# A fused scan-and-attention kernel: normalising the first chunk's second half sooner, and starting the projections ahead 22 slots later

## The chip, the cores and the metric

The kernel runs on one core of a Trainium2 chip. A core has a matmul engine (TensorE, PE in the views; its weight loads are PEld), a vector engine (VectorE, DVE), an activation engine (ScalarE, ACT), a general engine (GpSimd, POOL), and a queue engine (SyncE, SP) that mainly issues transfers. ACT issues transfers too. Each engine runs its own instructions in order and waits on semaphores for the others. The metric is the device time of the whole launch in microseconds (us).

## The reference

Input x has 32 sequences of 256 tokens with 256 features; a condition vector has 512 features for each sequence. First a selective scan is computed, then two layers of local attention and a gated feed-forward, and x is added at the end.

```python
xr, gate = split(x @ W_in.T)            # 512 + 512 channels
xc = silu(causal_conv4(xr + cond))      # per channel, along tokens
xn = layernorm(xc)                      # over the 512 channels
Bm, Cm, dt = split(xn @ W_xproj.T, 3)   # 16 states each
Ad = 1 - tanh(A_log) * 0.01 * tanh(dt @ W_dt.T + b_dt)
Bd = Bm * minimum(norm(xn), 1)
h  = clip(h * Ad + Bd * xn, -10, 10)    # one step for each token
y  = Cm . h + D * xn
x1 = (y * silu(gate)) @ W_out.T
x2 = two layers of attention and feed-forward on x1
out = x + x2
```

## The kernel before, in words

The 32 sequences are taken as NG = 4 groups of GB = 8. The scan of a group goes through NCH = 8 chunks of CH = 32 tokens. In a step of the scan (`step`, L722) DVE updates a 128 x 512 state h (16 states x 8 sequences on the partitions, 512 channels along a row) for one token of eight sequences. There are 256 steps for a group.

A chunk needs much before its first step. `project` (L401) multiplies x with the input weights, `conv_in` and `conv_taps` (POOL L480, DVE L474 and L491) do the convolution and `conv_th` (L501) the silu. `raw_sums` (L520) forms the raw B, C and dt sums. Then each chunk is normalised in NJ = 2 halves of 128 rows:

- `norm_turn` (PE L550) transposes a half into `tp_x`;
- `norm_stats` (DVE L560 to L569, POOL L567) takes mean and variance and raises the variance to the power -0.5;
- `norm_shift` and `norm_apply` (ACT L574, L581) write the normalised rows `xn`;
- `norm_affine` (POOL L588, L589) multiplies and adds the learnt scale and shift;
- `norm_put` (SP L599) writes the half to `xnd` in device memory; `norm_out` (ACT L594) sums the squares.

`length` (DVE L605, POOL L606) takes the norm of both halves, `figures` and `figures_out` (DVE L615, PE L624) spread the statistics, `figures_in` and `decays` turn them into the factors `beta`, the limits of the clip and so on. In the first group, rows for the steps come in two ways: `load_skip` (SP L751) loads `xq` from `xnd`, and `spread_rows` (PE L699) copies two of every eight tokens from it to all partitions as `bx`; the others are loaded by `load_rows` (SP L691), 256 KB each, as `xrep`. `scale_row` (ACT L712) multiplies by beta. `read_out` (PE L734) sums h with C for four tokens into `y`.

The scan of the first group runs nearly alone, before any attention. Beside it the kernel projects x for the later groups ("ahead"): 48 units u, each with `ahead_load` (SP L417, two transfers of 128 KB into `xa` for every second unit), `ahead_project` (PE L428, four matmuls into `ps_a`, eight rows of the profile), `ahead_copy` (ACT L439) and `ahead_put` (SP L444, 256 KB to `ahead`). From slot 220 or so they are all done, and later groups only load them (`xp`).

Order: each piece of work is put into a slot with `at(slot, what, ...)`. Slot 0 is the first step, and a step takes one slot. `scan_slots` runs the slots in order; within a slot one list comes before the other. The program is then built by a scheduling layer that may shift instructions of one engine past each other, so that a change of slots also moves other work, such as the weight loads (L985), which have no inputs to wait for. Once built, the order on each engine is fixed. A transfer uses one of eight semaphores in turn, so its issue can also wait for the transfer eight before it.

In the startup, small constants are folded too: `widen_w` (POOL L292) writes `wide`, `sum_w` (PE L303) sums it into `tw`, `sums_w` (DVE L312 to L314) copies `wsum` and `wbias`.

After slot 274 the first group is done, and attention and feed-forward of a group run beside the scan of the next group.

Of the kernel before, what the change touches and what calls it, by code (L numbers as in the profile page):

```python
# [27 lines left out]
CH = 32  # L28
NCH = S // CH
# [44 lines left out]
def kernel(  # L74
# [149 lines left out]
    def program(ctx, exact):  # L224
# [154 lines left out]
        def group_scan(g):  # L379
# [8 lines left out]
            alone = g == 0  # L388
# [5 lines left out]
            def at(s, what, *args):  # L394
                agendas[-1].setdefault(s, []).append(partial(what, *args))
# [289 lines left out]
            def by_tensor(t):  # L685
                return alone and t % (2 * NQ) < XR
# [175 lines left out]
            for c in range(NCH):  # L862
                s0 = c * CH
                for hb in range(CH // TB):
                    s = s0 + hb * TB
                    for i in range(NI):
                        at(s + 4 * i + 5, read_out, c, hb, i)
                    at(s + 21, gated, c, hb)
                    at(s + 25, out_gate, c, hb)
                    at(s + 11, skip, c, hb)  # L870
                for ch in range(NC_):
                    at(s0 - 38 + 2 * ch, conv_in, c, ch)
                    at(s0 - 37 + 2 * ch, conv_taps, c, ch)
                    at(s0 - 36 + 2 * ch, conv_th, c, ch)
                    if not alone:
                        at(s0 - 35 + 2 * ch, conv_out, c, ch)
                for ch, s in enumerate((13, 16, 17, 18)):
                    at(s0 + s + 2, gate_th, c, ch)
                    if not alone:
                        at(s0 + s + 4, gate_out, c, ch)  # L880
                at(s0 - 25, raw_copy, c)
                at(s0 - 24, raw_turn, c)
                for j in range(NJ):
                    s = s0 - 26 + 4 * j
                    at(s + 2, norm_stats, c, j)
                    at(s + 5, norm_shift, c, j)
                    at(s + 5, norm_apply, c, j)
                    at(s + 6, norm_affine, c, j)
                    at(s + 9, norm_out, c, j)
                    at(s + (9 if alone else 10), norm_put, c, j)  # L890
                at(s0 - 11, length, c)
                at(s0 - 9, figures, c)
                at(s0 - 7, figures_in, c)
                at(s0 - 6, decay_th, c)
                at(s0 - 5, decays, c)
                at(s0 - 4, put_c, c, 0)
                at(s0 + 4, put_c, c, 1)
                for d in range(KM):
                    at(s0 + 45 + 2 * d, copy_y, c, d)
                    at(s0 + 46 + 2 * d, put_y, c, d)  # L900
            agendas.append({})
            for c in range(NCH):
                s0 = c * CH
                at(s0 - 43 if alone else s0 + 6, load_x, c)
                if alone:
                    for ch in range(NC_):
                        at(s0 - 40 + 2 * ch, project, c, ch)
                else:
                    for i in range(2):
                        at(s0 - 44 + 2 * i, load_projected, c, i)  # L910
                for ch, s in enumerate((13, 16, 17, 18)):
                    at(s0 + s, project, c, NC_ + ch)
                at(s0 - 27, raw_sums, c)
                for j in range(NJ):
                    at(s0 - 26 + 4 * j, norm_turn, c, j)
                at(s0 - 8, figures_out, c)
                for t in range(CH):
                    if not by_tensor(t):
                        at(s0 + t - 6, load_rows, c, t)
                    if by_tensor(t) and t % XR == 0:  # L920
                        at(s0 + t - 4, spread_rows, c, t)
                    at(s0 + t - 2, scale_row, c, t)
                for hb in range(CH // TB):
                    s = s0 + hb * TB
                    at(s - 9 if alone else s + 7, load_skip, c, hb)
                    at(s + 23, out_turn, c)
                for d in range(KM):
                    at(s0 + 43 + 2 * d, project_y, c, d)

            if alone:  # L930
                n = (NG - 1) * NCH * 2
                for u in range(n):
                    s = -30 + u * (NCH * CH) // n
                    at(s - 5, ahead_load, u)
                    at(s, ahead_project, u)
                    at(s + 2, ahead_copy, u)
                    at(s + 4, ahead_put, u)
            return agendas

        def scan_slots(groups):  # L940


            slots, scans = {}, [group_scan(g) for g in groups]
            for part in range(2):
                for i, agendas in enumerate(scans):
                    for s, what in agendas[part].items():
                        slots.setdefault(i * S + s, []).extend(what)
            for s in range(min(slots), max(slots) + 1):
                for what in slots.get(s, ()):
                    what()  # L950
                yield s
# [613 lines left out]
        s0 = done[0]  # L1565
# [130 lines left out]
```

## Time and profile before

| | us |
|---|---|
| median of 3 runs | 3534.11 |
| lowest, highest | 3530.09, 3535.70 |
| the profiled execution | 3535.63 |
| its span, first to last instruction | 3533.5 |
| PE busy in the span | 3418.2 (97%) |
| DVE busy | 2683.2 (76%) |
| ACT busy | 2035.4 (58%) |
| POOL busy | 1625.6 (46%) |

The profile's page gives for each engine the time in which it was busy, the same in 40 slices, the DMA queues, the chain of waits followed back from the last instruction, and the costliest groups of instructions. A row such as `L722 DVE CUSTOM_DVE_ANT_0 h<-h,xrep,lim` names the line of the kernel, the engine, the operation, and output and inputs by their names in the program. In rows in order of time the first number is the start and the second the duration, both in us; `x4` counts instructions, and the bracket tells how long the engine was idle before and what ended that. `SPq` and `ACTq` are issues of transfers. Busy PE time is modelled in part, and a PE that waits between the parts of a matmul can count as busy.

### The profile page before, as it was taken

The numbers are of one execution on the slowest core, as the hardware profiler recorded it, in microseconds if no ns is written. First come the engines' busy times: TensorE is split into PE (matmuls) and PEld (weight loads), VectorE is DVE, ScalarE is ACT, GpSimd is POOL, SyncE is SP. The second block draws the span as 40 slices with busy tenths as digits, with TensorE's granted clock in tenths as the row PEclk, the third lists the DMA queues.
The fourth block names the chain that finished last, engine by engine and source line by source line (L and its number), as shares of the span: only waits on it lengthen the run. The fifth ranks groups of instructions, "written<-read, shape, count | busy, mean of one in ns | idle before, by whom it ended". The sixth has DMA issues, their size and how long they took to land.

```text
span 3533.5 us, 56484 instructions
## 1 busy us (share of the span) xinstructions
PE 3418.2 (97%) x19580; PEld 2257.4 (64%) x19580; DVE 2683.2 (76%) x5177; ACT 2035.4 (58%) x3663; POOL 1625.6 (46%) x1587
## 2 busy tenths in 40 slices
PE   7999989999999999999999999999999999999999
PEld 4545335666666666666666666666666777777777
DVE  5888898878788788888888888888787655555563
ACT  4666656656666665666666656666566444444442
POOL 4433456544455555544455555544444434333441
PEclk9999999999999999999999999999999999999999
DMA  7787655545454555444454555544444212011111
GB/s 208 215 217 218 198 169 153 136 113 142 129 143 130 150 147 151 136 114 134 117 142 128 148 148 147 137 120 130 118 142 118 61 37 62 13 31 36 37 28 38
DMA packets 487195, 436.65 MB, mean 124 GB/s; under 512 B 247155, under 2 KB 326516, under 8 KB 486772
## 3 DMA queue, kind: packets, MB, share of 16 engines
q1 hardware_dynamic: 401426, 420.41, 42.2%
q10 hardware_dynamic: 85474, 12.53, 2.1%
q8 instruction: 157, 2.57, 0.3%
q14 instruction: 138, 1.13, 0.1%
HBM read 384.06 MB, written 47.19 MB: 122 GB/s over the span
## 4 chain that ended last, share of the span: by engine, by line
PE 63%; DVE 17%; DMA 7%; POOL 5%; ACT 4%; issue 3%; SPq 1%; ACTq 0%; DVEq 0%; POOLq 0%
PE ps_qkv L996 13%; PE pa L1405 13%; DVE h L722 7%; PE po_f L1432 6%; PE y L734 5%; PE ps_wo L1052 4%; PE ov L1289 3%; DMA xrep<-xnd 3%; PE ps_out L814 3%; PE ps_in L401 3%; PE sc L1232 3%; PE tr_qk L1041 2%; PE rs L1269 2%; PE ps_raw L520 2%; DVE acc L491 1%
## 5 line engine op out<-in xcount | busy, mean ns | idle before, releaser
L722 DVE CUSTOM_DVE_ANT_0 h<-h,xrep,lim 128x512 f32<-128x512 f32 x1024 | 917.2, 896 | 137.3 <-ACT xrep L712 93.4
L712 ACT ACTIVATE xrep<-xrep,beta 128x512 f32<-128x512 f32 x960 | 671.6, 719 | 265.5 <-DMA xrep<-xnd 178.2
L996 PE MATMUL ps_qkv<-qkv,res 128*128 128x512 f32 x1536 | 716.0, 601 | 26.6 <-DVE ag L1423 12.5
L1405 PE MATMUL pa<-hT,w 128*128 128x256 f32 (+1 forms) x2816 | 674.7, 382 | 5.1 <-DVE zT L805 5.1
L1405 PEld LDWEIGHTS pa<-hT,w 128*128 128x128 f32 (+1 forms) x2816 | 517.4, 188 | 145.4 <-issue 41.8
L1020 POOL TENSOR_TENSOR rot<-rot,swp 128x512 f32<-128x512 f32 x256 | 345.1, 1348 | 496.7 <-DVE swp L1017 465.9
L996 PEld LDWEIGHTS ps_qkv<-qkv,res 128*128 128x128 f32 x1536 | 282.0, 191 | 311.5 <-issue 247.0
L1026 POOL TENSOR_TENSOR rn<-ss,neg_half 128x8 f32<-128x8 f32 x256 | 457.6, 1788 | 0.0
L734 PE MATMUL y<-h,ly 128*32 128x512 f32 x2048 | 341.1, 606 | 15.7 <-DVE h L722 13.6
L1432 PE MATMUL po_f<-ag,w 128*128 128x256 f32 x1280 | 306.7, 387 | 3.8 <-DVE fo L1443 3.1
L1423 DVE SCALAR_TENSOR_TENSOR ag<-pa,b_sb,ag 128x256 f32<-128x256 f32 x320 | 151.5, 474 | 208.7 <-ACT ag L1416 208.7
L1009 ACT ACTIVATE sq<-ps_qkv,tiny 128x512 f32<-128x512 f32 x256 | 173.3, 685 | 186.3 <-PE ps_qkv L996 129.3
L1432 PEld LDWEIGHTS po_f<-ag,w 128*128 128x128 f32 x1280 | 235.3, 190 | 68.3 <-DVE pT L1260 12.9
L1416 ACT ACTIVATE ag<-pa,b_sb 128x256 f32<-128x256 f32 x320 | 150.0, 469 | 209.7 <-PE pa L1405 206.8
L1357 POOL TENSOR_TENSOR rstd<-ve,neg_half 128x2 f32<-128x2 f32 x64 | 46.5, 726 | 484.9 <-DVE ve L1355 484.8
L1052 PE MATMUL ps_wo<-oT,wo 128*128 128x256 f32 x1024 | 231.6, 379 | 0.0
L1012 DVE TENSOR_TENSOR rot<-ps_qkv,rc_sb 128x512 f32<-128x512 f32 x256 | 175.1, 684 | 71.8 <-ACT sq L1009 70.1
L491 DVE SCALAR_TENSOR_TENSOR acc<-xr,wc_sb,acc 128x256 f32<-128x256 f32 x384 | 183.1, 499 | 50.8 <-POOL acc L480 50.0
L1017 DVE TENSOR_TENSOR swp<-ps_qkv,rs_sb 128x256 f32<-128x256 f32 x512 | 191.8, 416 | 27.6 <-POOL rot L1020 27.5
L1052 PEld LDWEIGHTS ps_wo<-oT,wo 128*128 128x128 f32 x1024 | 194.5, 190 | 27.2 <-ACT th_g L774 0.8
L1032 DVE SCALAR_TENSOR_TENSOR rot<-rn,rot 128x512 f32<-128x512 f32 x256 | 205.7, 841 | 7.5 <-POOL rn L1026 7.5
L1244 ACT ACTIVATE pT<-sc 128x512 f32<-128x512 f32 x384 | 201.6, 601 | 8.2 <-PE sc L1232 6.1
(161 smaller groups left out, 5375.6 us busy)
## 6 DMA issues: line engine op xcount, KB each, us to landing
xrep<-xnd SPq DMA_DIRECT2D x960, 256.0 KB
rb<-inv SPq DMA_DIRECT2D x128, 256.0 KB
xnd<-xn SPq DMA_DIRECT2D x64, 256.0 KB
qkv<-in_wqkv_dram SPq DMA_DIRECT2D x24, 512.0 KB
ahead<-xs_a SPq DMA_DIRECT2D x48, 256.0 KB
xp<-ahead SPq DMA_DIRECT2D x48, 256.0 KB
xd<-xnd SPq DMA_DIRECT2D x192, 64.0 KB
w<-in_w_dram SPq DMA_DIRECT2D x80, 128.0 KB
```

The costliest lines, as they stand in the source:

```text
L491: nc.vector.scalar_tensor_tensor(acc, xr[:, :, k : k + CH], wc_sb[:, ch, k : k + 1], acc, ALU.mult, ALU.add,)
L712: scaled = nc.scalar.activation(bx, ck[c].pop(("bx", t), bx), AF.Copy, scale=ck[c]["beta"][:, t : t + 1])
L722: nc.vector._custom_dve(TENSOR_ADD_SAT, out=h_new, in0=state["h"], in1=bx, s0=ck[c]["lim"][:, 0, t : t + 1], s1=ck[c]["lim"][:, 1, t : t + 1],
L734: nc.tensor.matmul(ck[c]["y", hb][32 * q : 32 * q + 32, :], ly[hb % 2][:, 32 * t : 32 * t + 32], ck[c].pop(("h", hb * TB + t)), start=(i = ...
L996: nc.tensor.matmul(ps, res[b][:, k, t0 : t0 + W], wt["qkv", a][:, k], start=(k == 0), stop=(k == KM - 1),)
L1020: nc.gpsimd.tensor_add(rot, rot, swp)
L1026: nc.gpsimd.tensor_tensor(rn, ss, neg_half, ALU.pow)
L1032: nc.vector.scalar_tensor_tensor(rot, bc(rn, 2, DH), 1e12, rot, ALU.min, ALU.mult)
L1052: nc.tensor.matmul(po[:, d], wt["wo", 0][:, c, d * P : (d + 1) * P], oT[:, c, :], start=(c == 0), stop=(c == NC_ - 1),)
L1244: nc.scalar.activation(p, banks[r], AF.Exp)
L1405: nc.tensor.matmul(dst[x], wt["w1", m][:, k, x], self.h[:, k], start=(k == 0), stop=(k == KM - 1),)
L1432: nc.tensor.matmul(self.po[:, d], wt["w2", 0][:, m, d * P : (d + 1) * P], self.ag[m], start=(m == 0), stop=(m == len(MCH) - 1),)
```

## The change

Two edits, both for the first group alone (`alone`):

1. In the first chunk (c = 0) the second half's normalisation is placed 1 slot behind the first half's, not 4. This moves `norm_turn`, `norm_stats`, `norm_shift`, `norm_apply`, `norm_affine`, `norm_out` and `norm_put` of j = 1 by 3 slots to the front.
2. The 48 units of projections ahead begin at slot -8, not -30, and are spread over 234 slots, not 256. Load, copy and put move with each unit.

```diff
                 for j in range(NJ):
-                    s = s0 - 26 + 4 * j
+                    s = s0 - 26 + (1 if alone and c == 0 else 4) * j
                     at(s + 2, norm_stats, c, j)
...
                 for j in range(NJ):
-                    at(s0 - 26 + 4 * j, norm_turn, c, j)
+                    at(s0 - 26 + (1 if alone and c == 0 else 4) * j, norm_turn, c, j)
...
                 n = (NG - 1) * NCH * 2
                 for u in range(n):
-                    s = -30 + u * (NCH * CH) // n
+                    s = -8 + u * (NCH * CH - 22) // n
                     at(s - 5, ahead_load, u)
                     at(s, ahead_project, u)
                     at(s + 2, ahead_copy, u)
                     at(s + 4, ahead_put, u)
```

In the built programs the order of instructions differs on every engine up to the end of the first group's scan and is the same after it.

## The prediction

> **What bounds the kernel now.** All times are from one profiled execution: 3535.63 us, of which the span from first to last instruction is 3533.5 us. The median of the three runs shown is 3534.11 us, so I work out a difference and add it to either; my forecast is given against the median.
>
> I read the page's slices first: TensorE is busy nine tenths everywhere but in the first 40 us and in the slice around 470 us. So the first scan (group 0, before attention starts near 490 us) has a start-up with idle engines and then a stretch in which TensorE is nearly full. The busy time by stretch shows both; the columns are from:to, length, then busy us and instructions of PE, PEld, DVE, ACT, POOL, then clock, DMA share and GB/s.
>
> ```profile
> 18.00:42.00 24.00, 19.73 (x111) 15.65 (x110) 7.53 (x23) 8.64 (x19) 12.48 (x20) 0.93 0.78 225
> 100.00:381.00 281.00, 266.82 (x1201) 145.98 (x1200) 243.81 (x417) 184.96 (x341) 109.12 (x144) 0.95 0.80 218
> ```
>
> The reader is to see 266.82 of 281 us of PE in the second row (95%), DVE at 87%, DMA at 80%. Who bounds it is told by the chain of waits of that window alone:
>
> ```profile
> by line: PE ps_a L428 15.1%; PE y L734 14.8%; DMA xrep<-xnd 10.6%; DVE h L722 9.5%; PE ps_in L401 9.1%; PE bx L699 7.8%; PE ps_out L814 6.8%; PE ps_raw L520 4.3%; issue 4.1%; ACT xrep L712 3.5%; DMA xq<-xnd 3.2%; PE tp_x L550 2.3%; DMA xp<-
> ```
>
> The seven PE terms sum to 60%; ps_a, the projection that the change moves, is the largest of all. Its rows before the first step (40) and in the full stretch (285):
>
> ```profile
> L428 PE MATMUL ps_a<-xa,w_in_sb x40: 379/379/483, 18.6 to 40.0; 128*128 128x256 f32 x40
> L428 PE MATMUL ps_a<-xa,w_in_sb x285: 379/379/634, 99.7 to 380.9; 128*128 128x256 f32 x143
> ```
>
> Eight rows are one unit u, so 5 units run before the first step and 36 in the stretch. The start-up, in order of time:
>
> ```profile
> 28.65 0.70 DVE L560 BATCH_NORM_STATS2 st<-tp_x 128x6 f32<-128x512 f32 x1 [3.72 <-PE tp_x L550]
> 31.89 0.63 PE L550 MATMUL tp_x<-ident,xc 128*128 128x128 f32 x4
> 33.17 1.97 PE L428 MATMUL ps_a<-xa,w_in_sb 128*128 128x256 f32 x8
> 34.88 0.61 POOL L292 COPY wide<-wx 128x512 f32<-128x512 f32 x1
> 37.20 1.26 POOL L588 TENSOR_TENSOR xn<-xn,lng_sb 128x512 f32<-128x512 f32 x1 [1.71 <-ACT xn L581]
> 38.55 1.26 POOL L589 TENSOR_TENSOR xn<-xn,lnb_sb 128x512 f32<-128x512 f32 x1
> 39.84 0.34 SPq L599 DMA_DIRECT2D xnd<-xn  x1
> 40.59 0.17 DVE L605 TENSOR_SCALAR ss<-ss 128x2 f32<-128x2 f32 x1 [3.31 <-ACT sq_x L594]
> 41.99 0.66 PE L624 MATMUL ps_st<-rhs,sel 128*128 128x96 f32 x4 [1.61 <-DVE rhs L615]
> 43.76 2.83 SPq L751 DMA_DIRECT2D xq<-xnd  x4
> 48.71 0.81 DVE L722 CUSTOM_DVE_ANT_0 h<-h,xrep,lim 128x512 f32<-128x512 f32 x1 [0.45 <-POOL xr L473]
> 48.75 2.08 PE L401 MATMUL ps_in<-xg,w_in_sb 128*128 128x256 f32 x4
> 52.95 1.03 PE L401 MATMUL ps_in<-xg,w_in_sb 128*128 128x256 f32 x4
> 53.00 0.80 DVE L722 CUSTOM_DVE_ANT_0 h<-h,xrep,lim 128x512 f32<-128x512 f32 x1
> ```
>
> It shows the first half's statistics at 28.65, the second half's transposes 3.2 us later at 31.89, the second half's row write at 39.84, its length at 40.59, the first step at 48.71 and the second at 53.00. The whole stretch counts: after the first scan the order of every engine is the same in both built programs, and PE is busy 2654 of 2700 us from 600 to 3300. What the first scan gains or loses moves the end by as much.
>
> **The change, part by part.**
>
> *Second half earlier.* In the built order the second transposes follow the first after one tw group (0.95 us), so they end at about 28.62 + 0.95 + 0.63 = 30.2 instead of 32.5. But the later engines serialise. DVE now does both bn_stats and both aggregates before either half's variance leaves: 30.2 + 0.70 + 2 x 0.18 + 0.15 + 0.14 + 0.15 = 31.7. POOL then does two powers (0.58 each), two wide copies (0.61 each) and four passes of 1.26 with gaps of 0.08: the passes start at about 33.9 and end at 39.2. So the first half's write slips from 34.43 to about 36.5, and the second's comes at 39.2 instead of 39.84: 0.6 us gained. The third wide copy, at 34.88 before, now stands behind the passes: 39.2 + 0.61, then its tw matmuls (0.95), then the three wsum copies (0.4), which stand ahead of the length on DVE. The length starts at about 41.3 instead of 40.59: 0.7 us **lost**. So what needs the figures (ps_st, beta) is 0.7 us late and the row write 0.6 us early.
>
> *Row loads.* The SP queue of before has 3.92 us between the second write (39.84) and xq (43.76); in the built order of before xq also waits for a matmul that reads an xa buffer, and in the new one it does not. I cost the gain from 0 (xq was not last) to 2.0 us. Then comes the first step: in the new DVE order it stands behind two taps of the next chunk's third channel, where the second step stood (53.00). So the first step gets later, about 52, and the next ones find their work done; by the fifth step (57.24) I count both orders as equal. Queued on SP ahead of the first write now are all weight loads, the 768 KB one included. Its price is 0 if it has landed by 36; six loads took 7.80 us at 23.40, so eight more issues at 1.3 us from 31 end at 41.4, 2.2 us after the write is due. Four small-run xa transfers and five 256 KB puts leave the same stretch, so I take 0. Start-up sum: from -4.0 (write 0.6, xq 2.0, and 1.4 from a lighter queue, that being xa's own issue of 8.99 us for six) to +2.9 (0.7 + 2.2); I take 0.
>
> *Projections later.* 48 units now lie 4.875 slots apart instead of 5.33, from slot -8. Five leave the idle start-up; in PE's order one of them stands between ps_st and the first bx, the rest among the steps. In 100 to 381 that is 36 x (5.333/4.875 - 1) = 3.4 units more, and 1.6 more between 42 and 100. Price of one: at most its whole 1.97 us, if PE never waits: 5 x 1.97 = 9.9 us. At least what a unit now adds to the chain: 15.1% of 281 us by 36 units is 1.18 us, and from 53 to 100 ps_a is 6.5% of the chain for 7 units, 0.44 us: 3.4 x 1.18 + 1.6 x 0.44 = 4.7 us. PE's 95% speaks for the upper end, its 60% of the chain for the lower; y and bx also count waits for h and xq as busy. I take the mean, **+7.3 us**. Each unit's ACT copy (0.57 us) and SP put move with it; I cost them at nothing here, since ACT is busy 185 of 281 us; if ACT were full they would add 5 x 0.57 = 2.9.
>
> *DMA.* Five puts (256 KB) and four xa loads (128 KB) enter the step time; the 768 KB and 42 KB weights leave it. That is 1.0 MB at 218 GB/s, 4.6 us of transfers; xrep and xq hold 13.8% of the chain: **+0.6 us**. Whole cost 4.6, if rows always ended last; 0 if never.
>
> Sum: 0 + 7.3 + 0.6 = **+7.9 us**, about 3543.5 for the profiled execution and 3542 for the median.
>
> [...]
>
> **Rivals.**
>
> *The start-up wins, not slower (-6 to +3.5).* Place: PE between bx and the ninth step. If write, xq and the clock all gain (-4.0 and up to 2.0 for bx and ps_in run warm) and extra units fall in PE's waits at 0.44 us each (2.2), the sum is -3.8: 3530. For it: PE idles 14 of 281 us, and y rows stretch while waiting for h. Against: ps_a heads the chain. It decides if the ninth step starts 3 us or more before its present 61 us.
>
> *Rows and order win, clearly faster.* xrep waits hold 10.6% of 281 us, 30 us. If the new order of puts and loads takes a third of them off, -10, with the rest at +3: 3527. For it: single waits of 5 us; against: more transfers in the stretch.
>
> *Everything is paid in full.* 9.9 for PE, 4.6 for DMA, 2.9 for the start: +17.4, 3551. For it: PE 95%, DMA 80%. Against: some of these overlap.
>
> *It does not do what it says:* the second half's figures come no earlier, since POOL and DVE serialise. That is in my forecast.
>
> **How the numbers follow.** Forecast +3.5 to +13: 0.52. Start-up wins: 0.27. Rows win: 0.13. Paid in full: 0.08. A difference of 0.2% (7.1 us, about what a measurement of this kernel can tell from no change) splits the forecast: 0.36 of it above. Faster by over 0.2%: 0.13 + 0.03 of the start-up case = 0.16. Slower: 0.36 + 0.08 = 0.44. Same: 0.40. The range leaves out about one in ten on each side: 3530 to 3549; the forecast's own is 3537 to 3547.
>
> **What would show it.** Right: no ps_a before about 43 us; second write near 39, length near 41; fifth step within 1 us of 57.2; then each 50 us holds about half a step less, PE busy over 96% from 100 to 381, the last ps_a near 389. Wrong: the ninth step well before 58, or the step rate unchanged at 1.52 us with more units in it (then units are free), or the end moving by other than the first scan's shift.

## The result and the profile after

The changed kernel takes 3547.23 us (median of 6 runs, 3543.48 to 3549.49), the kernel before 3531.64 us beside it (6 runs, 3530.09 to 3535.70): a ratio of 1.0036, with a 95% interval of 1.0024 to 1.0048, or 12.7 us more. The two medians alone lie 15.6 us apart, a quotient of 1.0044, which is inside that interval; the text goes by the ratio as recorded. The profiled execution took 3549.49 us, of which the span is 3547.2 us: 13.7 us more than the span of before.

The busy time by stretch, in the same columns as before:

```profile
18.00:42.00 24.00, 13.61 (x64) 11.17 (x64) 6.71 (x21) 5.40 (x13) 12.08 (x20) 0.63 0.69 200
100.00:381.00 281.00, 264.16 (x1197) 143.60 (x1196) 238.55 (x412) 181.84 (x335) 112.24 (x145) 0.98 0.82 216
```

In the start-up PE does 64 matmuls where it did 111, and the granted clock is 0.63 where it was 0.93. In the full stretch PE is busy 264.16 of 281 us; it was 266.82. The units are denser there, and yet PE is idle longer; but a second profile of the kernel before (before_again, below) has 262.77, so that difference is no more than lies between two executions of one kernel. The chain of waits of that stretch:

```profile
by line: PE ps_a L428 13.9%; PE y L734 13.4%; DMA xrep<-xnd 12.7%; DVE h L722 10.4%; PE ps_in L401 8.7%; PE ps_out L814 4.6%; issue 4.4%; PE bx L699 4.3%; ACT xrep L712 3.9%; PE ps_raw L520 3.8%; POOL acc L480 2.6%; PE tp_x L550 2.3%; DVE a
```

ps_a has less of the chain than before (13.9% after 15.1%), the row loads (xrep) and the steps (h) have more. This too is no effect of the change: in before_again, the same order as before, the same stretch has

```profile
by line: DMA xrep<-xnd 18.8%; DVE h L722 12.8%; PE ps_a L428 11.5%; PE y L734 10.7%; PE ps_in L401 6.6%; issue 4.7%; PE bx L699 4.5%; PE ps_out L814 4.1%; ACT xrep L712 4.0%; PE ps_raw L520 3.5%; DMA ys<-yo 3.3%; POOL acc L480 3.0%; DMA xq<
```

so even the line that heads the chain changes from one execution to the next. The units' rows, from 40 to 410 us, with the first and last start:

```profile
L428 PE MATMUL ps_a<-xa,w_in_sb x384: 379/379/634, 45.5 to 401.8; 128*128 128x256 f32 x192
```

No unit runs before 45.5, and the last ends near 402, 20 us later than before. The start-up in order of time (start, duration, and in brackets the idle time before and what ended it):

```profile
36.00 2.89 SPq L599 DMA_DIRECT2D xnd<-xn  x2
39.15 1.87 PE L303 MATMUL tw<-wx,wide 128*128 128x2 f32 x8 [2.67 <-POOL wide L292]
41.05 0.16 DVE L312 COPY wsum<-tw 128x3 f32<-128x3 f32 x1 [9.77 <-PE tw L303]
41.39 0.16 DVE L605 TENSOR_SCALAR ss<-ss 128x2 f32<-128x2 f32 x1
42.78 1.14 PE L624 MATMUL ps_st<-rhs,sel 128*128 128x96 f32 x4 [1.77 <-DVE rhs L615]
43.71 1.97 PE L401 MATMUL ps_in<-xg,w_in_sb 128*128 128x256 f32 x4
55.20 0.81 DVE L722 CUSTOM_DVE_ANT_0 h<-h,xrep,lim 128x512 f32<-128x512 f32 x1
```

The two row writes are issued as one group from 36.00; the last tw group takes 1.87 us instead of 0.95, and behind it stand wsum and the length, at 41.39; ps_st takes 1.14 us instead of 0.66, the first four rows of ps_in 1.97 instead of some 1.0; the first step is at 55.20.

Where the time went is read best from the starts of the steps (the rows of L722). Against the first profile of before the changed kernel is 3.5 us late at the ninth step, 6.6 at the 17th, 8.7 at step 184, 7.8 at step 204, 15.5 at step 224, and 14.4 at step 256. So the loss does not grow evenly with the steps; it comes at the start, between steps 12 and 16, and between steps 204 and 224. The end of the first scan carries it on: the first matmul of attention starts 15.4 us later, the span ends 13.7 us later.

### The profile page after: what moved, and what is told of

Read it like the earlier page. It is cut to its first block, busy times and chain, and to the rows that moved or that the text cites. A ratio compares the mean times of both kernels' runs of the same rounds, so it can differ in the third digit from the quotient of the medians.

```text
span 3547.2 us, 56509 instructions
## 1 busy us (share of the span) xinstructions
PE 3424.2 (97%) x19580; PEld 2257.8 (64%) x19580; DVE 2684.6 (76%) x5177; ACT 2037.2 (57%) x3663; POOL 1629.2 (46%) x1587
## 3 DMA queue, kind: packets, MB, share of 16 engines
q14 instruction: 138, 1.13, 0.1%
## 4 chain that ended last, share of the span: by engine, by line
PE 63%; DVE 17%; DMA 7%; POOL 5%; ACT 4%; issue 3%; SPq 0%; ACTq 0%; DVEq 0%; POOLq 0%
PE ps_qkv L996 14%; PE pa L1405 13%; DVE h L722 7%; PE po_f L1432 6%; PE y L734 5%; PE ps_wo L1052 4%; PE ov L1289 3%; DMA xrep<-xnd 3%; PE sc L1232 3%; PE ps_in L401 3%; PE ps_out L814 3%; PE tr_qk L1041 2%; PE rs L1269 2%; DVE acc L491 2%; PE ps_raw L520 2%
## 5 line engine op out<-in xcount | busy, mean ns | idle before, releaser
L722 DVE CUSTOM_DVE_ANT_0 h<-h,xrep,lim 128x512 f32<-128x512 f32 x1024 | 914.5, 893 | 142.8 <-ACT xrep L712 100.6
L734 PE MATMUL y<-h,ly 128*32 128x512 f32 x2048 | 356.3, 609 | 18.3 <-DVE h L722 17.6
```

The lines of the kernel that those rows point to most:

```text
L722: nc.vector._custom_dve(TENSOR_ADD_SAT, out=h_new, in0=state["h"], in1=bx, s0=ck[c]["lim"][:, 0, t : t + 1], s1=ck[c]["lim"][:, 1, t : t + 1],
L734: nc.tensor.matmul(ck[c]["y", hb][32 * q : 32 * q + 32, :], ly[hb % 2][:, 32 * t : 32 * t + 32], ck[c].pop(("h", hb * TB + t)), start=(i = ...
```

## The experiments

The names of the theories in the expectations: **A**, the cold TensorE clock of the start-up; **B**, my prediction's, that a unit among the steps is paid as PE time; **C**, that the loss is a matter of the order on the queues at a few places; **D**, that edit 1 loses the start. All runs are compared by ratio with the kernel before on the same chip, since its median there lay between 3531.64 and 3540.24 us. In one list, with the ratio turned into us by 3535:

| kernel | units: first slot, spread | ratio [95%] | us |
|---|---|---|---|
| after | -8, 234 | 1.0036 [1.0024, 1.0048] | +12.7 |
| after_again | -8, 234 | 1.0031 [1.0019, 1.0042] | +11.0 |
| warm | -8, 234 | 1.0035 [1.0023, 1.0047] | +12.4 |
| late_only | -8, 234 | 1.0023 [1.0012, 1.0033] | +8.1 |
| spread_238 | -8, 238 | 1.0025 [1.0014, 1.0036] | +8.8 |
| spread_252 | -8, 252 | 1.0027 [1.0017, 1.0036] | +9.5 |
| late_wide | -8, 256 | 1.0001 [0.9990, 1.0012] | +0.4 |
| dense_early | -30, 234 | 1.0022 [1.0013, 1.0031] | +7.8 |
| half_only | -30, 256 | 1.0000 [0.9991, 1.0009] | 0.0 |
| sparse_drift | -30, 278 | 1.0010 [0.9997, 1.0023] | +3.5 |
| before_again | -30, 256 | 1.0001 [0.9989, 1.0012] | +0.4 |
| put_act | -8, 234 | 1.0007 [0.9997, 1.0016] | +2.5 |
| before_put_act | -30, 256 | 0.9985 [0.9971, 1.0000] | -5.3 |

late_only, before_again and before_put_act have the second half of before (four slots), the others that of the change (one slot).

**Each edit alone.** half_only keeps edit 1 and takes edit 2 back:

```diff
-                    s = -8 + u * (NCH * CH - 22) // n
+                    s = -30 + u * (NCH * CH) // n
```

> Edit 1 alone: second half one slot behind the first, the 48 units as before (from slot -30, over 256 slots). Theory A (cold TensorE: without the five units between the start-up chains the clock falls, and each short chain is paid double): the units are back, so the start keeps its clock; ps_st near 0.7 us, the fifth step near 57.2 us, total within 2 us of the kernel before. Theory B (my prediction: five units that cost nothing in the start-up are paid among the steps): also within 2 us. Theory C (the late units meet the next group's loads near slots 184 to 220): also within 2 us. Rival D (the second half's passes push the last wide copy, wsum and with it the length back by 0.8 us, and that is the start's loss): fifth step 3 us late, total +3 or more.

Measured 1.0000: edit 1 alone costs nothing, and D falls. late_only has edit 2 without edit 1 (`s = s0 - 26 + 4 * j` in both places):

> Edit 2 alone: the second half stays four slots behind the first, the 48 units begin at slot -8 and are spread over 234 slots. Theories A, B and C: the whole loss is here, +10 to +15 us against the kernel before. Theory A adds: first ps_st over 1 us and granted clock under 0.7 from 18 to 42 us, fifth step 2 us late or more. Rival D (edit 1 is what loses the start): at most +9, and a fifth step near 57.2.

Measured +8.1 us, under the 10 to 15 that A, B and C had: some two thirds of the loss belong to edit 2 by this number, and the interval (4 to 12 us) reaches nearly all of it. It holds D's bound of 9 too, but half_only has settled D.

**The clock.** warm adds to the kernel after five units of matmuls whose result nobody reads:

```diff
+                for s in (-30, -25, -20, -15, -10):
+                    at(s, warm)
```

> The kernel after with five dummy units on TensorE alone at the slots that lost a unit (-30, -25, -20, -15, -10): eight rows each of the input weights by themselves into a bank that nobody reads; no transfer, no copy, and the outputs are not changed. Theory A: the clock from 18 to 42 us is back near 0.93, ps_st near 0.7, first ps_in near 1.0, fifth step near 57.2, and the total 3.5 to 6 us below the kernel after (3541 to 3544). Theories B and C: the start is not the cause, total as after (3546 to 3549). If the start's 3.3 us come from elsewhere (wsum behind the passes), step times up to the fifth are as in the kernel after.

The start came out as A has it, the total did not. The same stretches in warm:

```profile
18.00:42.00 24.00, 19.39 (x103) 15.15 (x103) 6.71 (x21) 6.14 (x14) 11.69 (x19) 0.86 0.65 192
42.00:53.00 11.00, 11.00 (x52) 8.88 (x51) 7.09 (x22) 3.18 (x7) 6.17 (x14) 1.00 0.62 160
```

The clock is back at 0.86 and 1.00, and the ninth step starts at 63.1 us. In the five profiles with edit 1, units from slot -8 and the puts on SP, but no filler, it starts at 64.2 to 66.5 (mean 65.6). But the whole kernel is at 1.0035, as the kernel after. So the cold clock costs some 2.5 us at the start, by one profile, and is not what costs 12.

**Density.** dense_early has the spacing of the change from the old first slot:

```diff
-                    s = -8 + u * (NCH * CH - 22) // n
+                    s = -30 + u * (NCH * CH - 22) // n
```

> Edit 1, and the units as dense as in the kernel after (one in 4.875 slots) but from slot -30, so that the last stands near slot 199. Five units stand in the start-up again. Theory B (PE is full, a unit among the steps is paid wherever it stands): about as before, -2 to +2. Theory C (late units collide with the next group's loads from slot 212): also no late loss, and rather faster than before, -2 to -6, since before has its last units at slot 220. If density itself were the loss (too many transfers and matmuls a step), steps 16 to 190 would each be slower, by up to 7 us in all, and given back after slot 199.

Measured +7.8 us. B and C both had it at before or better; only the case named last in the expectation, that density itself is the loss, had a loss of that size and place. Its profile loses 1.6 us at steps 12 to 16 and 8.0 from 16 to 184, nothing at 204 to 224, and gives 2.6 back from step 184 to 256, where that case had all of it given back. The next runs were chosen to part the number of units from the order. late_wide begins late but has the old spacing:

```diff
-                    s = -8 + u * (NCH * CH - 22) // n
+                    s = -8 + u * (NCH * CH) // n
```

> Edit 1, and the units from slot -8 but as far apart as in the kernel before (256 slots), so that they end at slot 242: five units stand in steps that had none, and no step has more than before. Theory B: the five are paid as in the kernel after, +7 to +12. Theory C: in the built order xp stands ahead of the xq loads, as in the kernel before, so the loss at steps 212 to 216 is gone; start +3, five units in steps that are not full of PE work about +2 (by 46.9 us for 32 steps without units against 48.4 with six, 0.25 each, to 0.44), total +4 to +6.

Measured 1.0001, or +0.4 us with an interval from -4 to +4: under C's 4 to 6, whose lower end it just reaches. Five units moved out of the start-up, to the steps behind slot 220, cost nothing that can be told. That is against B's +7 to +12 for five displaced units; it does not test the denser spacing, which late_wide does not have. spread_252 then changes one number of late_wide, 256 to 252, and with it the order on SP:

```diff
-                    s = -8 + u * (NCH * CH) // n
+                    s = -8 + u * 252 // n
```

> The kernel of run late_wide with 252 in place of 256: the units begin at slot -8 and lie 5.25 slots apart instead of 5.33, so the number of units in any stretch is the same to one, and the last stands at slot 238. In the built SP order, though, 50 xq loads stand ahead of the last chunk's x (xg) and 58 ahead of the next group's first xp, as in the kernel after (51 and 58); in late_wide and in the kernel before it is 48 and 56. Theory C (order on SP: x and xp come 3 steps late and PE and DVE, whose orders hold their readers, stand): the losses at steps 184 to 188 (+3) and 212 to 216 (+4 to +5) are there, total 6 to 9 us above late_wide, 1.0017 to 1.0026 of before. Theory B (so many units among the steps, each paid as PE time): as late_wide, 1.000 with 0.001 either way.

Measured 1.0027 against 1.0001, with intervals that do not touch: 9 us between two kernels whose unit counts are the same to one in any stretch. So 9 us can be lost without denser units. In the profiles 5.9 us of the difference come from step 204 to 224 (7.1 against 1.2), as C had it; the other loss that C forecast, at steps 184 to 188, is not there (0.2).

**Where the order costs: steps 212 to 216.** spread_238 changes 234 to 238 in the kernel after:

> The kernel after with one number changed: the 48 units from slot -8 are spread over 238 slots, not 234 (the last at slot 225, not 221). Up to slot 35 every unit stands where it stands in the kernel after; in the built order the next group's first load (xp) then stands on SP ahead of the xq loads of the last chunk but one, as it does in the kernel before, and not behind two of them. Theory C (the late loss is SP's order: xp is issued 3 steps later, and DVE, whose order holds the add of xp at step 216, waits 3.4 to 5.0 us for it where it waited 1.0): steps 212 to 216 take 6.6 us again, not 12, and the total falls by about 4, to 3542 to 3544. Theory B (each unit is paid as PE time wherever it stands among the steps): as the kernel after. The start should repeat that of the kernel after: +3 us at the fifth step, and the further 3.5 us at steps 12 to 16 if that is no accident of one execution.

The issues of SP around step 213, in the kernel before:

```profile
372.82 0.54 SPq L449 DMA_DIRECT2D xp<-ahead  x1
374.09 1.38 SPq L751 DMA_DIRECT2D xq<-xnd  x2
```

and in the kernel after:

```profile
383.75 1.36 SPq L751 DMA_DIRECT2D xq<-xnd  x2
385.21 0.39 SPq L449 DMA_DIRECT2D xp<-ahead  x1
385.66 1.29 SPq L751 DMA_DIRECT2D xq<-xnd  x2
```

xp, the first load for group 1, was issued after 213 steps and ahead of two xq loads; now it is issued after 216 steps and behind them. Its reader on DVE (xr, L474) stands behind step 216 in both orders. What DVE waited for it, from the waits of 320 to 400 us (total, times, longest), in this order: before, after, spread_252, spread_238, late_wide, put_act (the kernel after with the puts on ACT, below).

```profile
DVE xr L474 <- DMA xp<-ahead: 1.0, 1, 1.0
```

```profile
DVE xr L474 <- DMA xp<-ahead: 5.0, 1, 5.0
```

```profile
DVE xr L474 <- DMA xp<-ahead: 3.0, 1, 3.0
```

```profile
DVE xr L474 <- DMA xp<-ahead: 2.0, 1, 2.0
```

```profile
DVE xr L474 <- DMA xp<-ahead: 1.4, 1, 1.4
```

```profile
DVE xr L474 <- DMA xp<-ahead: 3.1, 1, 3.1
```

In the kernel after, 5.0 of the loss fall between the starts of the 216th and the 217th step, where this wait stands, and 1.0 in the next step. In spread_238, where xp again stands ahead of the two xq, steps 212 to 216 lose 1.0 us and not 5.4. Its total is 3.9 us under that of after and 2.2 under that of after_again, with intervals that overlap: the fall of 4 that C forecast is not told apart from none, and 8.8 us stay without this place. Nor is the wait by itself the price: put_act waits 3.1 us, as long as spread_252, and loses 1.7 us from step 204 to 224 where spread_252 loses 7.1. It has xp ahead of the two xq, and its reader one step sooner.

**Where the order costs: steps 12 to 16.** after_again runs the changed kernel a second time, before_again the kernel before.

> The kernel after once more, for a second profile of the same order: if the three local losses are made by the order and not by the one execution, steps 12 to 14, 184 to 188 and 212 to 216 again take 3 to 5 us longer than in the kernel before, and the total is 1.0024 to 1.0048 of before.

> The kernel before once more, for a second profile and as a measure of what the comparison can tell. The ratio should be 1.000 with 0.001 either way. In the profile: no loss at steps 12 to 14, 184 to 188 and 212 to 216 (within 1.5 us of the first profile each), x and xp waits under 1.5 us. What is open is the ninth step: 61.2 us in the first profile, 61.3 to 64.2 in kernels with units from slot -30, 64.2 to 66.5 in those with edit 1 and units from slot -8. If the second profile has it at 62 to 64, part of the start's loss in the kernel after is only that the first profile of before was early; if it is at 61 to 62, the start's loss is 3 to 5 us.

Both ratios came as expected. The ninth step of before_again did not: at 64.6 us it is later than either case had it, and as late as in the kernel after. The three local losses are there again in after_again (3.2, 3.1 and 4.5 us) and not in before_again (0.2, 0.2 and 0.3). The loss of 3 us at steps 184 to 188, where the last chunk's x (xg) is issued 3 steps late, is given back: from step 184 to 204 the kernel after gains 0.9 us, after_again 0.5. So two of the three last. The earlier of them is seen on POOL. In the kernel before, in order of time:

```profile
66.68 1.26 POOL L588 TENSOR_TENSOR xn<-xn,lng_sb 128x512 f32<-128x512 f32 x1 [1.78 <-ACT xn L581]
68.02 1.60 POOL L589 TENSOR_TENSOR xn<-xn,lnb_sb 128x512 f32<-128x512 f32 x1
69.58 0.55 POOL L567 TENSOR_TENSOR stat<-ve,neg_half 128x1 f32<-128x1 f32 x1
70.12 2.77 POOL L333 TENSOR_SCALAR w_out_sb<-w_out_sb 128x1024 f32<-128x1024 f32 x1
```

and in the kernel after:

```profile
71.49 1.27 POOL L588 TENSOR_TENSOR xn<-xn,lng_sb 128x512 f32<-128x512 f32 x1 [3.72 <-ACT xn L581]
72.71 0.55 POOL L567 TENSOR_TENSOR stat<-ve,neg_half 128x1 f32<-128x1 f32 x1
73.24 2.78 POOL L333 TENSOR_SCALAR w_out_sb<-w_out_sb 128x1024 f32<-128x1024 f32 x1
75.99 1.27 POOL L589 TENSOR_TENSOR xn<-xn,lnb_sb 128x512 f32<-128x512 f32 x1
```

The second half's power (0.55) and the one-time folding of the output weights (L333, 2.78) now stand between the two passes of the second chunk's first half. That is 3.3 us, and who waits for the second pass is told by ACT and by DVE:

```profile
77.28 0.63 ACT L594 ACTIVATE sq_x<-xn 128x512 bf16<-128x512 f32 x1 [2.88 <-POOL xn L589]
77.82 0.19 ACT L594 ACTIVATION_READ_ACCUMULATOR sq_x<-xn 128x1 f32 x1
77.91 0.71 ACT L712 ACTIVATE xrep<-xrep,beta 128x512 f32<-128x512 f32 x1
```

```profile
78.65 2.67 DVE L722 CUSTOM_DVE_ANT_0 h<-h,xrep,lim 128x512 f32<-128x512 f32 x2 [7.07 <-ACT xrep L712]
```

The same step in the kernel before, and in before_again:

```profile
72.02 2.68 DVE L722 CUSTOM_DVE_ANT_0 h<-h,xrep,lim 128x512 f32<-128x512 f32 x2 [3.40 <-ACT xrep L712]
```

```profile
75.72 2.67 DVE L722 CUSTOM_DVE_ANT_0 h<-h,xrep,lim 128x512 f32<-128x512 f32 x2 [4.74 <-ACT xrep L712]
```

The sum of squares (sq_x) stands ahead of the scaling of the next row (xrep), so the step waits 7.07 us and not 3.4 or 4.7. In the rows of ACT above, the 2.88 us of waiting stand ahead of sq_x, and the scaling behind it, which needs nothing from sq_x, starts only after it, at 77.91.

Neither a folded constant nor sq_x is touched by the diff. All profiles with the puts on SP together, in us against the first profile of before (step starts of L722), with what the built order says:

| kernel | ninth step | 12 to 16 | L333 between the passes | 16 to 184 | 204 to 224 | xq ahead of first xp |
|---|---|---|---|---|---|---|
| before | 0 | 0 | no | 0 | 0 | 56 |
| before_again | +3.4 | +0.2 | no | +2.9 | +0.5 | 56 |
| half_only | +2.9 | +0.2 | no | +3.9 | 0.0 | 56 |
| late_wide | +5.1 | -0.8 | no | +2.1 | +1.2 | 56 |
| sparse_drift | +2.0 | +0.1 | no | +1.4 | -0.9 | 56 |
| dense_early | +0.1 | +1.6 | yes | +8.0 | -1.1 | 56 |
| spread_238 | +3.0 | +3.4 | yes | +5.2 | +2.0 | 56 |
| spread_252 | +5.3 | -1.2 | no | +5.1 | +7.1 | 58 |
| late_only | +3.7 | -1.7 | no | -0.8 | +6.7 | 58 |
| warm | +1.9 | +1.5 | yes | +0.3 | +6.6 | 58 |
| after | +3.5 | +3.5 | yes | +2.1 | +7.6 | 58 |
| after_again | +5.3 | +3.2 | yes | +6.0 | +6.9 | 58 |

With 58 xq ahead of xp, steps 204 to 224 lose 6.6 to 7.6 us, in five profiles of five; with 56, -1.1 to +2.0, in seven of seven. With L333 between the passes, steps 12 to 16 lose 1.5 to 3.5, else -1.7 to +0.2. But L333 alone is not enough. In before_put_act (the kernel before with the puts on ACT, below) it stands between the passes too:

```profile
73.23 0.55 POOL L567 TENSOR_TENSOR stat<-ve,neg_half 128x1 f32<-128x1 f32 x1
73.76 2.78 POOL L333 TENSOR_SCALAR w_out_sb<-w_out_sb 128x1024 f32<-128x1024 f32 x1
76.51 1.31 POOL L589 TENSOR_TENSOR xn<-xn,lnb_sb 128x512 f32<-128x512 f32 x1
```

and steps 12 to 16 take 2.6 us less than in the first profile of before. There ACT scales three rows before it comes to sq_x:

```profile
74.17 1.34 ACT L712 ACTIVATE xrep<-xrep,beta 128x512 f32<-128x512 f32 x2 [2.25 <-DMA xrep<-xnd]
75.42 0.66 ACT L712 ACTIVATE xrep<-bx,beta 128x512 f32<-128x512 f32 x1
```

In dense_early and warm one row is scaled between the fold and sq_x, and they lose 1.6 and 1.5; in after, after_again and spread_238 none, and they lose 3.2 to 3.5. So the loss goes with both places together, and no run moved either alone.

**No fixed place in the chunk.** sparse_drift spreads the units over 278 slots from -30:

```diff
-                    s = -8 + u * (NCH * CH - 22) // n
+                    s = -30 + u * (NCH * CH + 22) // n
```

> Edit 1, and the units from slot -30 over 278 slots: 5.79 apart, none of them in step with the 32 slots of a chunk, the last at slot 242. In the built order 48 xq loads stand ahead of the last chunk's x and 56 ahead of xp, as in the kernel before. Theory C: no loss at steps 184 to 188 and 212 to 216, total within 2 us of before. Theory B: 8 per cent fewer units in steps 0 to 220, so 2 to 4 units leave the full stretch for steps that have room: 3 to 8 us faster than before. A third theory (units that drift through the chunk's pattern instead of keeping their place in it cost by themselves): 4 to 8 us slower than before.

Measured +3.5 us, with an interval from -1 to +8: B's gain of 3 to 8 us is not there, C's 2 us either way and the third theory's 4 to 8 both fit. Its profile loses 5.2 us between steps 224 and 232, where its last units meet the loads for group 1. So it tells little of the drift.

**The queue.** put_act and before_put_act move the units' puts to ACT's queue:

```diff
-                nc.sync.dma_start(out=d, in_=state.pop(("ta", u)))
+                nc.scalar.dma_start(out=d, in_=state.pop(("ta", u)))
```

> The kernel after with the units' puts issued by ACT, right behind the copy that they wait for, and not by SP, where row loads stand behind them. Theory C (late row loads are held up on the SP queue, behind puts that wait up to 2.1 us for ACT, and xp behind xq): the losses at steps 184 to 188 (3 us) and 212 to 216 (5 us) shrink, total 3539 to 3543. Theory B: as the kernel after, 3546 to 3549, or worse by ACT's issues (48 of some 0.05 to 0.6 us).

> The kernel before with the same move of the puts from SP to ACT. If puts on SP hold up rows throughout the scan (SP waited 3.6 us for ACT's copies from 326 to 344 alone), faster than before by 2 to 8 us; if they matter only where the late units meet the next group's loads, within 2 us of before.

put_act measured 1.0007, below the intervals of after and after_again: most of the loss against before goes, with the number and the slots of the units unchanged. In its built order 56 xq stand ahead of the first xp, and L333 ahead of both passes; its profile loses 1.7 us from step 204 to 224 and gains 2.8 from 12 to 16, while the loss at steps 184 to 188 stays (3.8). before_put_act measured 0.9985, with an interval that just touches 1 and a median 2 us under that of before: a small gain at most, though surely faster than the kernel after.

But the puts on ACT may help any kernel, so put_act is better held against before_put_act, which differs from it by the two edits alone and was measured on the same chip against the same runs. The ratios lie 0.0022 apart, or 7.8 us, and the medians (3544.01 and 3537.15) 6.9. So with the puts on ACT the edits still cost some 7 us, though both places are out of the comparison: from step 12 to 16 the two kernels gain 2.8 and 2.6, from 204 to 224 they lose 1.7 and 1.8. In their profiles put_act is 3.0 us later at the ninth step and loses 3.2 more from step 16 to 184, where its units are denser. The two places in the order are therefore not the whole loss.

## Why the prediction was near, and in part by luck

- **What bounds the kernel, and that the end moves with the first scan:** the second is right. The first matmul of attention is 15.4 us late and the end 13.7; after step 256 nothing is lost or gained beyond what two runs of one kernel differ by. That ps_a heads the chain held for the one execution that was read; in before_again the row loads head it, with 18.8%.
- **Second half earlier:** the times on the engines were right (second write at about 38.6 for a forecast 39.2, length 41.39 for 41.3, the last tw group behind the passes). That it "does not do what it says", since POOL and DVE serialise, was right too: half_only is at 1.0000.
- **Start-up 0, from -4.0 to +2.9:** the size of the chosen value was off: the sum has no price for a slower clock ahead of the first step. The granted clock from 18 to 42 us fell from 0.93 (0.86 in before_again) to 0.63 (0.61 in after_again), and the last tw group (1.87 us, 0.95 in before), ps_st (1.14, 0.66) and the first four rows of ps_in (1.97, some 1.0) took nearly twice as long; over these rows the clock was 0.50, in before 1.00. In return the first bx took 1.13 us, in before 2.07, and the four ps_in rows behind it 1.13, in before 2.08 at a clock of 0.50: 1.9 us for the two, where the first rival had up to 2.0. Over bx itself the granted clock was 0.91 in before and 1.00 after, so that the clock made bx's part is not shown. The ninth step is at 65.6 us in the mean of five profiles with units from -8 (64.2 to 66.5), and at 62.9 in the mean of five with units from -30 (before, before_again, half_only, sparse_drift, dense_early; 61.2 to 64.6): +2.7 us. That the fifth step would be "within 1 us of 57.2" was wrong by the first profile (60.6), but before_again has 60.7: one profile is not enough to set such a mark.
- **Projections later, +7.3:** this term is neither confirmed nor refuted, and it stood in for losses of another kind. Its price rested on PE's share of the chain in one execution: 15.1% for ps_a, 1.18 us a unit. In before_again, the same order, the share is 11.5%, which gives 0.92 us by the 35 units there. From step 16 to 184 there are some 3 units more (168/4.875 less 168/5.333), by the prediction's prices 3.5 to 5.8 us. The mean of six profiles with spacings of 4.875 or 4.958 (after, after_again, late_only, warm, dense_early, spread_238) is 3.5 us there, that of four with 5.333 (before, before_again, half_only, late_wide) 2.2: a price of 1.3 us. But the single values run from -0.8 to 8.0, spread_252 at 5.25 has 5.1, and the pair with the puts on ACT differs by 3.2, so a price like the forecast's lower end is not excluded. That PE would be busy over 96% was wrong (94%), and the last ps_a, forecast near 389, came at 402.
- **DMA, +0.6:** not told apart.
- **What the term left out:** two places in the built order, which the sum had at nothing. In the profiles of the kernel after, L333 between two passes, with sq_x right behind, goes with 3.3 us, and xp behind two xq with about 7 from step 204 to 224. With 2.7 of the start and 1.3 of density that is 14.3, less about 1 that is given back behind step 224, for 12.7 and 11.0 measured. The sum is of local losses and need not hold for the total: spread_238 has xp in its old place and still loses 8.8. That +7.9 came near is partly luck, since the order was not in the forecast.
- **The rivals:** "Rows and order win" had named the mechanism, the order of puts and loads, but only as a gain of 10. An order that a scheduling layer makes can fall either way, and the reasoning in it gave no ground for the sign. "Everything is paid in full" had 17.4, as far above the measured 12.7 as the forecast lies below it, from prices at their upper ends.
- **What stays open:** how much is density. All kernels with spacings of 4.875 or 4.958 and the puts on SP lose 7.8 to 12.7 us, and of those with 5.25 and more only spread_252 loses over 3.5. dense_early (7.8) and spread_238 (8.8) have xp in the old place, and with the puts on ACT some 7 us remain; only late_wide and spread_252 part the order from the density. Whether edit 1 adds to edit 2 (12.7 and 11.0 against 8.1) is within the intervals, though the one profile of late_only has no L333 between the passes. Why xp behind two xq goes with 7 us when DVE's wait grew by 4 is followed only in part: 1.0 falls in the next step and 1.4 to 2.2 in steps 204 to 208, ahead of the wait.

## What to carry to other kernels

Where a scheduling layer makes the order, an edit is not only what the diff moves: compare the built order queue by queue, look for loads that now stand behind others and for one-time work that has slipped between two steps of a chain, and price those places too. Before a loss is put down to the number of instructions, change the spacing by a hair (256 to 252): if the time jumps while the count stays, the count is not all. If a remedy for the order helps, try it on the kernel before as well, and compare the two. And take a second profile of the same kernel before reading 3 us, or a share of the chain, out of one.

## What the runs showed of the hardware that was not expected

Work without a purpose kept the clock up: with five units of dummy matmuls the granted clock from 18 to 42 us was 0.86 and not 0.63, and from 42 to 53 it was 1.00 and not 0.72. Two profiles of one kernel, taken at different times, differed by 3.4 us (before) and 1.7 us (after) at the ninth step, and by 2.9 and 3.9 us from step 16 to 184, with the same order of instructions.
